# One layer of an eight-layer transformer kernel: last-token thoughts with features on partitions, token norms moved into the attention before, gates moved ahead of the thoughts

## The chip, the cores and the metric

The kernel runs on one core of a Trainium2 chip. The metric is the device time of one launch in microseconds (us), median over runs. All data is 32-bit floating point.

## What is computed

Eight layers on `x` of 4 batches x 256 tokens x 256 features, each added to `x` after a norm of it: cross-attention and feed-forward, four times (`a0 f0 a1 f1 a2 f2 a3 f3`). The change lies in `f1`, the second feed-forward layer, where a "thought" is made of each batch's last token and broadcast to all its tokens:

```python
def layer_norm(x, gamma, beta):
    mu = jnp.mean(x, axis=-1, keepdims=True)
    var = jnp.mean(jnp.square(x - mu), axis=-1, keepdims=True)
    return (x - mu) * jax.lax.rsqrt(var + EPS) * gamma + beta
x_norm = layer_norm(x, in_gamma, in_beta)
thought = x_norm[:, -1, :] @ agg_w + agg_b          # 4 x 256
for _ in range(4):
    t = layer_norm(thought, pn_gamma, pn_beta)
    t = gelu(t @ d1_w + d1_b)                        # 4 x 1024
    thought = thought + (t @ d2_w + d2_b)
broadcast = (thought @ bc_w + bc_b)[:, None, :]
gate = jax.nn.sigmoid(x @ gate_w + gate_b)
return layer_norm(x + gate * broadcast, out_gamma, out_beta)
# the caller: x = x + f1(_layernorm(x))
```

## The kernel before

The kernel is written on a tile framework. It places the tiles, sets every semaphore, and orders each engine's instructions ahead of time: a planner walks the program with its own cost estimates and gives an idle engine the first instruction, in the order of the source, that it thinks is ready. So the source order is a priority, later work fills gaps in earlier work, and the order is fixed before the chip runs. A tile of a pool waits until the memory, or the rotating buffer of its tag, is free.

`x` is held as eight tiles of 128 tokens x 256 features (two per batch), tokens on partitions. PSUM has 4 banks `work`, 3 `held` and one `longest`.

**The attention `a1`, before `f1`.** It goes through 4 batches x 16 heads x 2 token tiles. TensorE makes scores (`sc`), VectorE their maxima and ScalarE the exponentials, VectorE scales them, TensorE transposes them (`tp_a1p`) and multiplies with the context (`pv`) and the output weights (`o_a`, line 853). `finish` and `pair` trail the scores; `pair` is a generator in the list `left`, one step of which is taken per unit. At a batch's last head `pair` adds the batch's output to `x` (`add_to_x`, line 240).

**The layer `f1`.** Its weights (`f1w` with agg, bc and gate, `f1d1`, `f1d2`) are loaded long before. Then, in the order of the source:

1. Eleven vector loads (biases, gammas, betas; line 156), on 4 partitions for the thoughts and on 128 for the tokens.
2. `normed` normalizes all eight tiles (`normalizing`: two statistics instructions, `rsqrt` with a VectorE scale at line 177 and a GpSimd power at line 178, and one scaling at line 203) and transposes each into `xnT` (line 210).
3. Four small DMAs (line 1108) bring the four last tokens as rows to partitions 0 to 3 (`last`).
4. `layer_norm` on a 4 x 256 tile, `columns` (two transposes and a copy: features to partitions), the product with `agg`: `thought`, 4 x 256.
5. Four steps, each: `layer_norm`, `columns`, d1 (16 products that each hold a 128x128 block of weights and move 4 columns), bias (line 1140), Gelu (line 1145), d2 (8 products that hold 128x4 activations and move 256 columns of weights), two additions (1149, 1150).
6. The thought's columns, and per batch `same`, the product `bc` and `spread` (1160); per tile the gate's product, its bias (1165) and sigmoid (1166), then eight more VectorE steps (1168, 1169, the norm of `layer_norm` with 1112 and 1113, and 1171, the addition to `x`).

TensorE makes each 32-bit product in two passes, so two records of the trace are one product; a transpose is one record.

Between these stand the `weight_products` of the next attention `a2`: 28 short steps (`products`) on its weights, drawn with `drain(products, n)`: 4 behind each of the five norms of thoughts and 2 in each step between d1 and d2. A step is four transposes (of wk, wq, wv), or four products 128x128 (`a2wqk`), or one product of 512 columns (`a2wvo`), and a copy out of PSUM. Their weights come through two rotating buffers by DMA.

`a2` begins with `begin(0)`, which normalizes batch 0 again (`bn_a`, `xn_a`, `tp_a`), and then queries (`q_a`).

Of the kernel before, what the change touches and what calls it, by code (L numbers as in the profile page):

```python
# [10 lines left out]
F32 = mybir.dt.float32  # L11
# [43 lines left out]
class Model:  # L55
    def __init__(self, ctx: ExitStack, tc: tile.TileContext, aps, out, layers):
# [10 lines left out]

        self.early = ctx.enter_context(ExitStack())
        self.weights = self.early.enter_context(tc.tile_pool(name="weights", bufs=3))

        self.normal = ctx.enter_context(ExitStack())
        self.n_copies, self.kinds = 0, dict(work=("work", 4), held=("held", 4))
# [137 lines left out]
            self.nc.tensor.transpose(ps[:, n * w : (n + 1) * w], block, self.ident[:w, :w])  # L210
        self.copy(out, ps[:, : len(blocks) * w].rearrange("p (n w) -> p n w", w=w))

    def normed(self, tag, keep=None):

        xnT = []
        for c in range(NCH):
            xT = self.acts.tile([P, NK, CH], F32, tag="xnT", name=f"xnT_{tag}_{c}", bufs=2)
            for i in range(CH // P):
                n = c * (CH // P) + i
                if keep is None:  # L220
                    xn = self.acts.tile([P, D], F32, tag="xn", name=f"xn_{tag}_{n}", bufs=3)
                else:
                    xn = keep.tile([P, D], F32, tag="xn_kept", name=f"xn_{tag}_{n}", bufs=NT)
                    self.kept.append(xn)
# [405 lines left out]
    def f0(self):  # L630
# [5 lines left out]
        wg = self.load(self.w8([P, NK, I], "f0wg"), aps["L0_ffn_w_gate"].rearrange("(k p) n -> p k n", p=P))  # L636
        wu = self.load(self.w8([P, NK, I], "f0wu"), aps["L0_ffn_w_up"].rearrange("(k p) n -> p k n", p=P))
        wd = self.load(self.w8([P, NI, D], "f0wd"), aps["L0_ffn_w_down"].rearrange("(k p) n -> p k n", p=P))
        self.a1w = self.a1_weights()
        with tc.tile_pool(name="f0", bufs=2) as p, tc.tile_pool(name="f0a", bufs=1) as self.acts:  # L640
            xnT = self.normed("f0")
# [114 lines left out]
    def a1(self):  # L756
# [7 lines left out]
        NI = S // P  # L764
        wk, wv, wq, wvo, g = self.a1w
        self.share_banks(4)
        with self.tc.tile_pool(name="a1", bufs=2) as p:
            nc.vector.tensor_scalar_mul(g[:, 0:1], g[:, 0:1], 1.0 / math.sqrt(HD))

# [71 lines left out]
            def pair(b, h, wT):  # L841
# [235 lines left out]
        self.staging.close()  # L1077


    def f1(self):  # L1080
        nc, aps, tc = self.nc, self.aps, self.tc
        HID, STEPS = 1024, 4
        NH = HID // P
        EPS = 1e-6
        w = self.w8([P, 3, NK, D], "f1w")
# [3 lines left out]
        d2 = self.load(self.w8([P, NH, D], "f1d2"), aps["L1_ffn_d2_w"].rearrange("(k p) n -> p k n", p=P))  # L1089
        with tc.tile_pool(name="f1c", bufs=1) as cp, tc.tile_pool(name="f1", bufs=2) as p, tc.tile_pool(  # L1090
            name="f1st", bufs=2
        ) as st, tc.tile_pool(name="f1a", bufs=1) as self.acts:
            products = self.weight_products(st, "a2")
            self.ready.add("a2")
            rows = {}
            for name in ("in_gamma", "in_beta", "agg_b", "pn_gamma", "pn_beta", "d2_b"):
                rows[name] = self.load(cp.tile([B, D], F32, name=name), row(aps[f"L1_ffn_{name}"], B))
            for name in ("bc_b", "gate_b", "out_gamma", "out_beta"):
                rows[name] = self.load(cp.tile([P, D], F32, name=name), row(aps[f"L1_ffn_{name}"], P))
            d1b = self.load(cp.tile([P, NH], F32, name="d1b"), aps["L1_ffn_d1_b"].rearrange("(n p) -> p n", p=P))  # L1100

            self.kept = []
            xnT = self.normed("f1", keep=cp)
            xn = self.kept

            last = cp.tile([B, D], F32, name="last")
            for b in range(B):
                nc.sync.dma_start(last[b : b + 1, :], xn[(b + 1) * (S // P) - 1][P - 1 : P, :])

            def layer_norm(out, x, gamma, beta, name):  # L1110
                self.normalize(out, x, EPS, name)
                nc.vector.tensor_tensor(out, out, gamma, ALU.mult)
                nc.vector.tensor_tensor(out, out, beta, ALU.add)

            def columns(x, name):
                xT = p.tile([P, NK, B], F32, tag="xT", name=f"xT_{name}")
                self.transposed(xT, [x[:, k * P : (k + 1) * P] for k in range(NK)], name)
                return xT

            t = p.tile([B, D], F32, tag="t", name="t_in")  # L1120
            layer_norm(t, last, rows["in_gamma"], rows["in_beta"], "f1in")
            drain(products, 4)
            tT = columns(t, "f1in")
            thought = cp.tile([B, D], F32, name="thought")
            ps = self.held("agg")
            self.matmuls(ps[:B, :D], [(tT[:, k, :], w[:, 0, k, :]) for k in range(NK)])
            nc.vector.tensor_tensor(thought, ps[:B, :D], rows["agg_b"], ALU.add)
            for step in range(STEPS):
                t = p.tile([B, D], F32, tag="t", name=f"t_{step}")
                layer_norm(t, thought, rows["pn_gamma"], rows["pn_beta"], f"f1_{step}")  # L1130
                drain(products, 4)
                tT = columns(t, f"f1_{step}")
                ps = self.held(f"d1_{step}")
                for n in range(NH):
                    self.matmuls(
                        ps[:, n * B : (n + 1) * B],
                        [(d1[:, k, n * P : (n + 1) * P], tT[:, k, :]) for k in range(NK)],
                    )
# [12 lines left out]
            drain(products)  # L1151
            thT = columns(thought, "f1th")
            for b in range(B):

                same = p.tile([P, NK, P], F32, tag="same", name=f"same_{b}")
                nc.vector.tensor_copy(same, thT[:, :, b : b + 1].to_broadcast([P, NK, P]))
# [4 lines left out]
                for i in range(b * (S // P), (b + 1) * (S // P)):  # L1161
                    ps = self.work(f"gate_{i}")
                    self.matmuls(ps[:, :D], [(self.tokens(xnT, k, i * P, P), w[:, 2, k, :]) for k in range(NK)])
                    gate = p.tile([P, D], F32, tag="gate", name=f"gate_{i}")
                    nc.vector.tensor_tensor(gate, ps[:, :D], rows["gate_b"], ALU.add)
                    nc.scalar.activation(gate, gate, AF.Sigmoid)
                    o = p.tile([P, D], F32, tag="o", name=f"o_{i}")
                    nc.vector.tensor_tensor(o, gate, spread, ALU.mult)
                    nc.vector.tensor_tensor(o, o, xn[i], ALU.add)
                    layer_norm(o, o, rows["out_gamma"], rows["out_beta"], f"f1o_{i}")  # L1170
                    nc.vector.tensor_tensor(self.x[i], self.x[i], o, ALU.add)


    def clean_rows(self, p):
# [651 lines left out]
```

## Time and profile before

| | |
|---|---|
| median of 7 runs | 2581.31 us (2572.13 to 2584.39) |
| the profiled execution | 2581.88 us, span 2580.1 us |
| TensorE busy | 2402.8 us, 93% of the span |
| VectorE, ScalarE, GpSimd busy | 51%, 35%, 15% |
| mean granted TensorE clock | 0.938 |
| end of `a1`: its last addition to `x` starts | 1093.05 us |
| first `thought` (line 1127) | 1111.80 us |
| the thoughts' last addition (line 1150) ends | 1181.93 us |
| first query product `q_a` of `a2` | 1215.14 us |

The span runs from the first to the last instruction of the profile. "Busy" of TensorE counts pipelined products whose ends are modelled, so a busy TensorE need not be at its peak. The granted clock is the share of full speed that TensorE's throttle let through. Windows are given in us from the span's start. In a window's row each engine has its busy time and its number of instructions, PE is TensorE, PEld its weight loads, DVE VectorE, ACT ScalarE, POOL GpSimd, SP the queue that issues the DMAs.

### The profile page before, as it was taken

The page shows a single profiled execution, that of the slowest core. Times are in us where ns is not written, and L with a number is a line of the kernel's source. Part 1 is how long each engine was busy: PE and PEld are TensorE (multiplying, and loading weights), DVE is VectorE, ACT ScalarE, POOL GpSimd, SP SyncE. Part 2 cuts the span into 40 slices and gives each one's busy share as a digit, 9 for nine tenths or more (in the row PEclk, how much of TensorE's full clock was granted, in tenths as well). Part 3 has the DMA queues.
Part 4 walks back from the last instruction along what each step waited for, and adds up shares of the span by engine and source line. Part 5 has one row for each costly group of instructions (what it writes and reads, how often), then busy time and mean ns, then how long its engine had stood idle before and what let it go on. Part 6 is the DMA issues. An engine that isn't in the chain of part 4 may idle for free. (4 is left out here: it accounts for less than half of the span.)

```text
span 2580.1 us, 27636 instructions
## 1 busy us (share of the span) xinstructions
PE 2402.8 (93%) x9742; PEld 1436.2 (56%) x9742; DVE 1319.1 (51%) x3502; ACT 896.2 (35%) x1886; POOL 399.7 (15%) x412
## 2 busy tenths in 40 slices
PE   5999999898999999986999999898879999999999
PEld 3454545464555555553666666587746565654444
DVE  5453442686666666535566766311255666552111
ACT  2323322225555555411444344132334343431111
POOL 6303200002212121101001201100120201002222
PEclk8887875899999999977999999999989999999999
DMA  8400000200000000022200000199720000005111
GB/s 258 139 1 1 1 1 1 98 29 17 1 1 1 1 1 1 1 85 57 53 2 25 25 1 25 60 271 245 233 92 2 25 7 20 1 1 168 49 53 41
DMA packets 102422, 134.91 MB, mean 52 GB/s; under 512 B 8272, under 2 KB 82760, under 8 KB 101768
## 3 DMA queue, kind: packets, MB, share of 16 engines
q1 hardware_dynamic: 97672, 120.51, 15.7%
q0 software_dynamic: 4608, 12.59, 1.5%
q8 instruction: 79, 1.29, 0.2%
q14 instruction: 63, 0.52, 0.1%
HBM read 96.50 MB, written 36.57 MB: 52 GB/s over the span
## 5 line engine op out<-in xcount | busy, mean ns | idle before, releaser
L170 PE MATMUL pv_a<-PT_a,ctx 128*128 128x512 f32 x768 | 350.8, 600 | 4.8 <-DVE f3taken L1570 2.9
L998 DVE CUSTOM_DVE_ANT_0 pr_a<-sc_a,mask_a 128x512 f32<-128x512 f32 x256 | 176.2, 688 | 199.8 <-PE sc_a L170 199.3
L170 PE MATMUL sc_a<-ctxT,qT_a 128*128 128x512 f32 x512 | 261.6, 595 | 0.8 <-DVE sm_a L998 0.8
L170 PEld LDWEIGHTS pv_a<-PT_a,ctx 128*128 128x128 f32 x768 | 141.3, 190 | 189.4 <-issue 152.8
L999 ACT ACTIVATE pr_a<-pr_a,sm_a 128x512 f32<-128x512 f32 x256 | 185.0, 723 | 119.3 <-DVE sm_a L998 95.4
L178 POOL TENSOR_TENSOR rstd_f<-rs_f,half 128x1 f32<-128x1 f32 (+1 forms) x36 | 19.5, 568 | 880.0 <-DVE rs_f L177 679.9
L1004 DVE TENSOR_SCALAR pr_a<-pr_a,sm_a,valid_a 128x512 f32<-128x512 f32 x256 | 140.3, 551 | 5.9
L1461 DVE TENSOR_TENSOR h<-u,gs 128x512 f32<-128x512 f32 x48 | 33.2, 691 | 205.5 <-POOL gs L1459 205.2
L170 PE MATMUL sc_a<-kT,qT 128*128 128x512 f32 x256 | 131.2, 597 | 1.7 <-ACT qT L791 1.7
L170 PE MATMUL st<-qTm,a0kT 17*128 17x256 f32 x512 | 119.3, 544 | 11.6 <-ACT pT L573 10.1
L170 PE MATMUL sc_a<-a0kT,a0qz 128*128 128x496 f32 x256 | 123.7, 605 | 0.0
L517 DVE TENSOR_REDUCE a0pad<-sc_a 128x1 f32<-128x496 f32 x128 | 85.8, 672 | 72.9 <-PE sc_a L170 72.5
L825 ACT ACTIVATE pr_a<-sc_a,sm_a 128x512 f32<-128x512 f32 x128 | 87.8, 687 | 95.0 <-DVE sm_a L824 93.7
L178 POOL TENSOR_TENSOR rr_a1k<-rs_a1k,half 128x4 f32<-128x4 f32 x64 | 64.5, 1008 | 327.4 <-DVE rs_a1k L177 272.1
L165 DVE COPY xTb_f<-tp_xb_f 128x256 f32<-128x256 f32 x79 | 33.5, 424 | 141.6 <-PE tp_xb_f L210 141.6
L170 PEld LDWEIGHTS st<-qTm,a0kT 17*128 17x128 f32 x512 | 71.8, 254 | 58.8 <-ACT pT L573 36.9
L573 ACT ACTIVATE pT<-st 128x512 f32<-128x512 f32 x128 | 69.4, 594 | 95.4 <-PE st L170 95.1
L1458 ACT ACTIVATE gs<-g 128x512 f32<-128x512 f32 x48 | 28.7, 597 | 209.4 <-PE g L170 209.4
L210 PEld LDWEIGHTS tp_a3p<-ident,pr_a 128*128 128x128 f32 x512 | 63.9, 141 | 65.2 <-issue 50.0
L987 ACT COPY qT_a<-q_a 128x512 f32<-128x512 f32 x64 | 37.5, 586 | 178.1 <-PE q_a L170 178.1
L210 PEld LDWEIGHTS tp_a2p<-ident,pr_a 128*128 128x128 f32 x512 | 63.9, 141 | 61.8 <-issue 47.4
L210 PEld LDWEIGHTS tp_a1p<-ident,pr_a 128*128 128x128 f32 x512 | 63.8, 141 | 53.3 <-issue 44.6
(487 smaller groups left out, 4688.3 us busy)
## 6 DMA issues: line engine op xcount, KB each, us to landing
sent<-zero SPq DMA_DIRECT2D x6, 2048.0 KB
f2w<-in_L_w1T_dram SPq DMA_DIRECT2D x16, 704.0 KB
f2w<-in_L_w2T_dram SPq DMA_DIRECT2D x16, 704.0 KB
xb_f<-sent SPq DMA_DIRECT2D x20, 512.0 KB
back<-yb_f SPq DMA_DIRECT2D x20, 512.0 KB
cb_f<-f3comb SPq DMA_DIRECT2D x32, 192.0 KB
cb_f<-f3comb SPq DMA_DIRECT2D x32, 128.0 KB
f3wg<-in_L_wgT_dram SPq DMA_DIRECT2D x3, 1024.0 KB
```

Of the source, the lines that this page charges most:

```text
L165: self.nc.vector.tensor_copy(out, in_)
L170: self.nc.tensor.matmul(out, lhsT, rhs, start=n == 0, stop=n == last)
L178: self.last_pow = self.nc.gpsimd.tensor_tensor(out, t[:p, :n], self.half[:p, :n], ALU.pow).ins
L210: self.nc.tensor.transpose(ps[:, n * w : (n + 1) * w], block, self.ident[:w, :w])
L517: nc.vector.tensor_reduce(pad[:, h, HD : HD + 1], ps[:, :MAIN], AX.X, ALU.max, negate=True)
L573: nc.scalar.activation(pT[:, j], ps[j].rearrange("p (n t) -> p n t", n=2), AF.Exp)
L825: nc.scalar.activation(pr, ps, AF.Exp, bias=st[:, 0:1], accum_out=st[:, 1:2])
L987: nc.scalar.copy(qT, ps.rearrange("p (m t) -> p m t", m=2))
L998: nc.vector.tensor_tensor_reduce(pr, ps, mask, -1.0, -3 * NEG, ALU.add, ALU.min, accum_out=st[:, 0:1])
L999: nc.scalar.activation(pr, pr, AF.Exp, bias=st[:, 0:1], scale=-1.0, accum_out=st[:, 1:2])
L1004: nc.vector.tensor_scalar(pr, pr, st[:, 0:1], valid, ALU.mult, ALU.mult)
L1461: nc.vector.tensor_tensor(h, pu, t, ALU.mult)
```

## The change

- `f1_room`, called in `f0`, makes a pool that lives until the end of `f1`, with `xnT` and the eight normalized tiles. `f1_vectors`, called at the start of `a1`, loads the vectors: seven as columns (features on partitions), four as rows on 128 partitions.
- `f1_tokens(b)` normalizes and transposes batch `b`. For batches 0 to 2 it is put behind the last `pair` of the batch in `a1`'s list `left`; batch 3 follows at the start of `f1`.
- The gates (product, bias, sigmoid) of tiles 0 to 5 come before the transposes of batch 3, those of tiles 6 and 7 right behind; all are kept.
- The last tokens are copied out of `xnT` as columns by two VectorE copies; the four DMAs go.
- Thoughts have the form 128 x 2 x 4. A norm takes two pairs of products with a matrix of ones (sum, sum of squares, on every partition) in the place of the statistics instructions, and 2 product steps of `a2` behind each pair; `columns` goes. `agg` and d2 hold blocks of weights and move 4 columns, as d1 does. d2's bias is added before d2.
- `out_beta` is added to `x` by GpSimd before the thoughts; the last norm becomes two fused VectorE instructions.

```diff
...
+    def f1_tokens(self, b):
+        nc, NI = self.nc, S // P
+        self.f1_done.add(b)
+        xn = self.f1_xn[b * NI : (b + 1) * NI]
+        yield from self.normalizing_all(xn, b, f"f1_{b}")
...
+                nc.tensor.transpose(ps[:, k, i * P : (i + 1) * P], xn[i][:, k * P : (k + 1) * P], self.ident)
+        yield
+        self.copy(self.f1_xnT[c][:, :, at : at + S], ps)
+        yield
...
@@ a1, pair
+                    if b + 1 < B:
+                        left.append(self.f1_tokens(b))
...
@@ f1
-            self.kept = []
-            xnT = self.normed("f1", keep=cp)
-            xn = self.kept
-            last = cp.tile([B, D], F32, name="last")
-            for b in range(B):
-                nc.sync.dma_start(last[b : b + 1, :], xn[(b + 1) * (S // P) - 1][P - 1 : P, :])
-            def layer_norm(out, x, gamma, beta, name):
-                self.normalize(out, x, EPS, name)
-                nc.vector.tensor_tensor(out, out, gamma, ALU.mult)
-                nc.vector.tensor_tensor(out, out, beta, ALU.add)
...
+            def gate(i):
+                ps = self.work(f"gate_{i}")
+                self.matmuls(ps[:, :D], [(self.tokens(xnT, k, i * P, P), w[:, 2, k, :]) for k in range(NK)])
+                nc.vector.tensor_tensor(gates[i], ps[:, :D], rows["gate_b"], ALU.add)
+                nc.scalar.activation(gates[i], gates[i], AF.Sigmoid)
...
+            def sums(x, name):
+                ps = self.held(f"sums_{name}")
+                self.matmuls(ps[:, :B], [(self.ones, x[:, k, :]) for k in range(NK)])
+                return ps[:, :B]
+            def layer_norm(x, gamma, beta, name):
+                ps = sums(x, f"m_{name}")
+                drain(products, 2)
+                d, sq, t = tile_("d", name), tile_("sq", name), tile_("t", name)
+                nc.vector.scalar_tensor_tensor(d, each(ps), -1.0 / D, x, ALU.mult, ALU.add)
+                nc.vector.tensor_tensor(sq, d, d, ALU.mult)
+                ps = sums(sq, f"v_{name}")
+                drain(products, 2)
+                r = self.stats.tile([P, B], F32, tag="rr", name=f"rr_{name}")
+                self.rsqrt(r, ps, 1.0 / D, EPS, name)
+                nc.vector.tensor_tensor(d, d, over(gamma), ALU.mult)
+                nc.vector.tensor_tensor(t, d, each(r), ALU.mult)
+                nc.vector.tensor_tensor(t, t, over(beta), ALU.add)
+                return t
+            tokens = self.f1_tokens(B - 1)
+            drain(tokens, 2)
+            for i in range(NT - NI):
+                gate(i)
+            drain(tokens)
...
+            for i in range(NT - NI, NT):
+                gate(i)
+            for i in range(NT):
+                nc.gpsimd.tensor_tensor(self.x[i], self.x[i], rows["out_beta"], ALU.add)
...
+                nc.vector.tensor_tensor(thought, thought, over(cols["d2_b"]), ALU.add)
                 drain(products, 2)
                 ps = self.held(f"d2_{step}")
-                self.matmuls(ps[:B, :D], [(act[:, n, :], d2[:, n, :]) for n in range(NH)])
-                nc.vector.tensor_tensor(thought, thought, ps[:B, :D], ALU.add)
-                nc.vector.tensor_tensor(thought, thought, rows["d2_b"], ALU.add)
+                for f in range(NK):
+                    self.matmuls(
+                        ps[:, f * B : (f + 1) * B], [(d2[:, n, f * P : (f + 1) * P], act[:, n, :]) for n in range(NH)]
+                    )
+                nc.vector.tensor_tensor(thought, thought, by_half(ps), ALU.add)
...
-                    layer_norm(o, o, rows["out_gamma"], rows["out_beta"], f"f1o_{i}")
-                    nc.vector.tensor_tensor(self.x[i], self.x[i], o, ALU.add)
+                for i, o, mv, r in halves:
+                    nc.vector.scalar_tensor_tensor(o, o, mv[:, 0:1], rows["out_gamma"], ALU.subtract, ALU.mult)
+                    nc.vector.scalar_tensor_tensor(self.x[i], o, r, self.x[i], ALU.mult, ALU.add)
+        self.told.close()
```

More of the change, by code (lines that the diff above doesn't have):

```diff
@@ L766, in a1 @@
         self.share_banks(4)
+        self.f1_vectors()
         with self.tc.tile_pool(name="a1", bufs=2) as p:
@@ L1093, in f1 @@
             products = self.weight_products(st, "a2")
             self.ready.add("a2")
[L1095 to L1100, printed above, removed]
@@ L1115, in columns @@
[L1115 to L1124, printed above, removed]
-            ps = self.held("agg")
@@ L1126, in f1 @@
-            self.matmuls(ps[:B, :D], [(tT[:, k, :], w[:, 0, k, :]) for k in range(NK)])
-            nc.vector.tensor_tensor(thought, ps[:B, :D], rows["agg_b"], ALU.add)
+            gates = [cp.tile([P, D], F32, name=f"gate_{i}") for i in range(NT)]
+            def gate(i):
[3 more added lines that the diff above has]
+                nc.scalar.activation(gates[i], gates[i], AF.Sigmoid)
@@ new lines, in f1 @@
+            for i in range(NT):
+                nc.gpsimd.tensor_tensor(self.x[i], self.x[i], rows["out_beta"], ALU.add)
+            t = layer_norm(last, cols["in_gamma"], cols["in_beta"], "f1in")
+            thought = cp.tile(few, F32, name="thought")
+            ps = self.held("agg")
+            for f in range(NK):
+                self.matmuls(
+                    ps[:, f * B : (f + 1) * B], [(w[:, 0, k, f * P : (f + 1) * P], t[:, k, :]) for k in range(NK)]
+                )
+            by_half = lambda ps: ps[:, : NK * B].rearrange("p (f b) -> p f b", b=B)
@@ L1128, in f1 @@
+            nc.vector.tensor_tensor(thought, by_half(ps), over(cols["agg_b"]), ALU.add)
             for step in range(STEPS):
[L1129 to L1132, printed above, removed]
+                t = layer_norm(thought, cols["pn_gamma"], cols["pn_beta"], f"f1_{step}")
                 ps = self.held(f"d1_{step}")
@@ L1160, in f1 @@
                 nc.vector.tensor_tensor(spread, ps[:, :D], rows["bc_b"], ALU.add)
[L1161 to L1169, printed above, removed]
-                    layer_norm(o, o, rows["out_gamma"], rows["out_beta"], f"f1o_{i}")
-                    nc.vector.tensor_tensor(self.x[i], self.x[i], o, ALU.add)
+                halves = []
+                for i in range(b * NI, (b + 1) * NI):
+                    o = gates[i]
+                    nc.vector.tensor_tensor(o, o, spread, ALU.mult)
+                    nc.vector.tensor_tensor(o, o, self.f1_xn[i], ALU.add)
+                    bn = self.stats.tile([P, 6], F32, tag="bn", name=f"bn_f1o_{i}")
+                    mv = self.stats.tile([P, 2], F32, tag="mv", name=f"mv_f1o_{i}")
+                    r = self.stats.tile([P, 1], F32, tag="rstd", name=f"rstd_f1o_{i}")
+                    nc.vector.bn_stats(bn, o)
+                    nc.vector.bn_aggr(mv, bn)
+                    self.rsqrt(r, mv[:, 1:2], 1.0, EPS, f"f1o_{i}")
+                    halves.append((i, o, mv, r))
+                for i, o, mv, r in halves:
+                    nc.vector.scalar_tensor_tensor(o, o, mv[:, 0:1], rows["out_gamma"], ALU.subtract, ALU.mult)
+                    nc.vector.scalar_tensor_tensor(self.x[i], o, r, self.x[i], ALU.mult, ALU.add)
+        self.told.close()
     def clean_rows(self, p):
```

58 lines of the change are left out of this document (48 added, 10 removed).

## The prediction

> **What bounds the kernel now.** First the page's slices of 64.5 us: TensorE (PE) is at 9 tenths nearly everywhere, so elsewhere only PE work counts. Slices 17 and 18 (counted from 0; 1097 to 1226 us) dip to 8 and 6, at a granted clock of 7 tenths.
>
> ```profile
> PE   5999999898999999986999999898879999999999
> PEclk8887875899999999977999999999989999999999
> ```
>
> Second, the windows by stage: attention `a1`; its end to the first thought; the four steps; output to the first query of `a2`.
>
> ```profile
> core 0: us, PE busy (x) PEld busy (x) DVE busy (x) ACT busy (x) POOL busy (x), PEclk, DMA share, GB/s
> 650.00:1093.00 443.00, 432.54 (x1701) 252.10 (x1699) 295.18 (x685) 221.71 (x457) 84.25 (x88) 1.00 0.00 1
> 1093.00:1111.80 18.80, 10.90 (x42) 6.34 (x41) 11.05 (x35) 2.83 (x7) 2.66 (x5) 0.58 0.48 137
> 1111.80:1181.50 69.70, 64.31 (x316) 41.79 (x317) 18.61 (x50) 13.70 (x25) 2.12 (x4) 0.79 0.17 50
> 1181.50:1215.10 33.60, 12.43 (x49) 8.79 (x47) 28.88 (x110) 3.50 (x8) 6.28 (x12) 0.70 0.06 14
> ```
>
> Row 1: PE is full (432.5 of 443), VectorE (DVE) has a third free. Row 2: nobody is full; the thought waits for a chain of norm, DMAs and norm. Row 3: PE is nearly full, at clock 0.79. Row 4: DVE is the bound.
>
> Third, the clock inside a step, windows and then PE's timeline:
>
> ```profile
> 1116.90:1119.90 3.00, 3.00 (x30) 3.00 (x29) 0.28 (x1) 1.88 (x2) 0.00 (x0) 1.00 0.48 169
> 1119.90:1123.30 3.40, 3.40 (x18) 3.40 (x18) 0.53 (x2) 0.68 (x2) 0.00 (x0) 0.50 0.00 0
> 1123.30:1126.70 3.40, 3.40 (x12) 1.57 (x11) 0.69 (x1) 0.74 (x2) 0.00 (x0) 0.50 0.32 81
> 1126.70:1130.10 3.40, 3.40 (x20) 1.77 (x18) 0.82 (x2) 0.00 (x0) 0.00 (x0) 0.99 0.18 74
> ```
> ```profile
> 1116.86 4.04 PE L170 MATMUL d<-xT_f,f1d 128*128 128x4 f32 x32
> 1120.76 2.05 PE L170 MATMUL a2wqk<-a2wkT,a2wqT 128*128 128x128 f32 x8
> 1122.61 1.92 PE L210 MATMUL tp_a2wq<-ident,a2wq 128*128 128x128 f32 x8
> 1124.45 4.73 PE L170 MATMUL d<-f1d,act 128*4 128x256 f32 x16
> ```
>
> d1, products that move 4 columns, fills PE without a gap from 1116.86, yet at 1119.9 the clock halves. d2, which moves 256 columns, starts at 1124.45 and has it back at 1126.7. The trace's starts give the price: records of d1 come every 0.112 us at full clock, 0.213 at half; of d2 every 0.216 and 0.427. The clock changes on a grid of 3.41 us (1113.1, and two and four such stretches later 1119.9 and 1126.7). A cold stretch turned warm with 2.25 of its 3.41 us in products of 256 columns (1123.3 to 1126.7), not with 1.85 in 128-column products and 0.7 in transposes (1119.9 to 1123.3). All three other stretches filled by d1 dropped the clock too.
>
> **The change, part by part**, against the profiled execution's 2581.88 us (span 2580.1), 0.57 over the median.
>
> *Tokens in the attention.* Three batches put 12 transposes on a full PE: 12 x 0.11 (record spacing, full clock) = 1.3 us; with a wait now and then +1.6 (0.5 to 4). Their norms (per tile statistics 0.41 + 0.17, scale 0.15, scaling 0.41) take 7 us on DVE, copies and powers 2 and 3 us: free in row 1. Eleven loads move to SP at `a1`'s start, 0.3 to 0.4 us of issue each; nothing behind them is wanted for 400 us. Without that cover they would cost the 4.8 us that they take now (1093.08 to 1097.75). GpSimd (POOL) adds `out_beta` eight times, 0.81 us each by the 128x256 row at L454; six fit in `a1`, two (1.6 us) lie before the first norm's power while POOL idles.
>
> *Attention's end to the first thought*, now 1093.05 to 1111.80 = 18.75 us. After: gates 0 to 5 on a warm PE, 6 x 4 x 0.216 = 5.2 us, over batch 3's norm on DVE (ready at 3.5); transposes, copy 0.6 and `last` to 6.7; gates 6 and 7, 1.7, to 8.2. They stand ahead of the thoughts in PE's queue, so the first sums wait for them. The norm and `agg`: 16 small records 1.8, links off PE 2.6, two pairs of transpose steps 1.8 less 0.6 hidden: 5.6 warm, up to 2.5 more cold. First thought at 13.8 warm; I take 13.9, since the gates have just kept the clock up. Gain 4.85 (2 to 5.5). The products' weights are now asked for at 0, not 7.9, and land in time (3.9 us for `a2wk`).
>
> *The four steps*, 1111.80 to 1181.93 = 70.1. New PE work per step: 8 records of sums, 32 of d1, 32 of d2, all moving 4 columns: 72 x 0.112 = 8.1 warm, 72 x 0.213 = 15.3 cold. d2 alone costs what it did (16 x 0.216 against 32 x 0.112), but no longer moves 256 columns. Links off PE, from small rows (128x32 addition 0.19, Gelu 0.23, scale 0.14): addition 0.25; difference and square 0.44; scale, power and two operations 1.77; bias and Gelu 0.53; four waits for a product's end at 0.18: 3.7. The power is on 128x4 now, 1.01 us, not 0.53:
>
> ```profile
> L178 POOL TENSOR_TENSOR rr_a1q<-rs_a1q,half 128x4 f32<-128x4 f32 x32 | 32.2, 1007 | 106.8 <-DVE rs_a1q L177 101.3 <-DVE rs_a L177 5.5
> L178 POOL TENSOR_TENSOR rstd_f<-rs_f,half 4x1 f32<-4x1 f32 x4 | 2.1, 531 | 60.0 <-DVE rs_f L177 60.0
> ```
>
> So a bare step is 11.8 warm, 19.0 cold. 24 product steps stand in the four: 32 transposes (0.11 / 0.213), 64 records of `a2wqk` (0.112 / 0.213), 16 of `a2wvo` (0.43 / 0.99 as seen): 17.6 warm, 36.2 cold. Of that 11 to 12 hide in the links; the rest stands ahead of the next sums, d1 or d2 in PE's queue. All warm: 47 + 17.6 - 11 = 54. All cold: 76 + 36.2 - 12 = 100. The same sum with the old records gives 53 and 95; the measured 70.1 lies 59% of the way to warm.
>
> Which clock? Only `a2wqk` and `a2wvo` can raise it now: eight pairs of steps, each about 3.4 us cold. One that starts anywhere on the grid has 2.25 us in one stretch in 2 x (3.41 - 2.25) / 3.41 = 68% of cases, and buys one warm stretch, worth 3.41 less the links' share: 2.9. 8 x 0.68 x 2.9 = 16, so 84. Two more for copies of products that sit ahead of the chain on DVE (0.5 us a step now, as the 0.69 us copy at 1114.65 before L1113): 86. Cost 15.9; ends 75 (each pair raises it for a full 3.41) and 102 (none does).
>
> Here a rule can be weighed. The Trainium skill, "TensorE: Matmul & The Clock Gate", Part 1 (The HAM clock gate), has the clock halve after about 3.4 us without PE activity and advises against idle gaps. The grid agrees; "idle" does not, since PE was busy 3.00 of 3.00 us before the drop. By the rule a PE full of small products would stay warm and the steps would take 54 + 2, a gain of 14; I go by the row.
>
> *Output.* DVE now, 1184.5 to 1212.6:
>
> ```profile
> L1171 DVE TENSOR_TENSOR x<-x,o 128x256 f32<-128x256 f32 x8 | 3.3, 416 | 0.0
> L1112 DVE TENSOR_TENSOR o<-o,out_gamma 128x256 f32<-128x256 f32 x8 | 3.3, 414 | 0.0
> L1165 DVE TENSOR_TENSOR gate<-gate,gate_b 128x256 f32<-128x256 f32 x6 | 2.4, 401 | 0.0
> ```
>
> Such instructions of 0.41 start 0.335 apart. Per tile four (L203, L1112, L1113, L1171) become two fused ones; the fused row at L1244 takes 0.48, I put 0.40 (0.335 to 0.48) apart: 4 x 0.335 - 2 x 0.40 = 0.54, x 8 = 4.3. Six gate biases go: 2.0. The thought's transposes and copy go (1.0), a cold first `bc` takes half back: 0.5. Gain 6.8 (5 to 9); after it the start of `a2` is late next, as now.
>
> **Sum:** +1.6 - 4.85 + 15.9 - 6.8 = +5.85: 2587.7, less 0.57 for the median: **2587**.
>
> **The rivals.** About 0.2% (5.2 us) is what a measurement of this kernel can tell from no change.
>
> *The clock stays up (faster).* The mechanism: pairs of products, or gates which the planner pulls into the steps as it now does at 1174.96, raise the clock in nearly every stretch. It decides where the steps take under 75 us, 27 of the 46 between cold and warm. For it: `a2wvo` pairs move 512 columns and follow each other in step four. Against: a 128-column run of 1.85 us failed, and gates stand first. Price: 2557 (all warm) to 2576, typically 2572.
>
> *Paid back exactly (same).* 17 to 27 of the 46 saved, steps 75 to 85: 2576 to 2586, middle 2581. Nothing in the rows excludes that six pairs of eight land well on a grid whose phase I do not know.
>
> *Small products leave the clock cold (slower).* My case: steps over 85. With no raise at all and an attention 4 us longer, 2605. That tokens in `a1` delay `pair` more than 4 us would add to it; row 1 has 10 us idle in 443, so some is absorbed.
>
> **How the numbers follow.** Slower 0.5, same 0.3, faster 0.2: I trust the count of cold records, less how the pairs fall. My case's own range is 2587 to 2604. Over all, 2570 to 2604: below, long raises with the better ends of attention and output (steps 75: -5; ends -5); above, one raise in eight.
>
> **What would show it.** Right: records of d2 0.213 apart with a granted clock of 0.5 to 0.7 in the steps; first thought 14 us after the last addition of `a1`; thoughts 82 to 90 us; last `x` some 20 us after the last thought; `a1` 1 to 2 us longer. Wrong: a clock of 0.79 or more in the steps, or d2 records 0.112 apart throughout, or an attention longer by over 5 us.

## The result, and the profile after

The median after is 2591.87 us (19 runs, 2581.76 to 2598.77) beside 2581.31 before (45 runs): a ratio of 1.0043 with a 95% interval of 1.0033 to 1.0054, so 8.5 to 13.9 us slower. The profiled execution took 2592.74 us (span 2591.0) against 2581.88.

The page's slices first, in tenths, 64.8 us each: PE is at 9 and 7 tenths in slices 17 and 18 now, while the clock is still down there, at 7 and 6.

```profile
PE   5999999898999999997999999898869999999999
PEclk7897875899999999976999999999989999999999
```

The windows by stage, cut at the same events as those of before (attention, its end to the first thought, the four steps, output to the first query of `a2`):

```profile
core 0: us, PE busy (x) PEld busy (x) DVE busy (x) ACT busy (x) POOL busy (x), PEclk, DMA share, GB/s
650.00:1105.40 455.40, 437.88 (x1721) 257.26 (x1720) 303.51 (x702) 223.12 (x461) 90.41 (x97) 0.99 0.00 1
1105.40:1119.00 13.60, 12.13 (x80) 10.78 (x79) 11.03 (x35) 6.05 (x12) 3.55 (x5) 1.00 0.43 145
1119.00:1197.00 78.00, 75.37 (x387) 66.92 (x386) 10.97 (x45) 11.08 (x20) 4.04 (x4) 0.65 0.16 45
1197.00:1221.70 24.70, 7.82 (x20) 4.83 (x20) 22.14 (x88) 0.59 (x1) 7.26 (x13) 0.60 0.14 43
```

Against the stages before (18.75, 70.1 and 33.2 us) the start is 5.2 shorter, the steps are 7.9 longer at a clock of 0.65, and the output is 8.6 shorter. The three batches of the attention between the first and the last addition to `x` took 125.9 + 126.0 + 105.1 us before and take 128.6 + 131.0 + 108.7 now. With 1.1 us before any of the moved work, the attention ends 12.4 us later.

12.4 - 5.2 + 7.9 - 8.6 = 6.5. The other 4.3 of the profiled 10.9 lie behind the first query: from the end of `a2` to the first addition of `a3` it takes 6.6 us longer (386.0 before, 392.6 after), and what follows takes some 2.5 less. In the fourteen traces of this study this stretch is 379.7 to 392.8 long, with nothing of the change in it and no order by kernel, so it is laid to the single execution. The medians are 8.5 to 13.9 us apart all the same. What 6.5 lacks is probably in the attention: the five other kernels that keep it as it is after the change (3, 8, 9, 11 and 12 below) take 371.6 us for the three batches, not 368.4, and 6.5 + 3.2 = 9.7.

**Where the attention waits.** PE's timeline behind the second batch turn (start, duration, line, tiles; in brackets the idle time and its releaser):

```profile
873.67 0.60 PE L1112 MATMUL tp_f<-ident,f1xn 128*128 128x128 f32 x4
874.11 0.60 PE L211 MATMUL tp_a1p<-ident,pr_a 128*128 128x128 f32 x4
877.78 1.11 PE L789 MATMUL t_a1q<-ident,nrm_a1q 128*128 128x128 f32 x4 [3.08 <-DVE nrm_a1q L783]
```

PE idles 3.08 us for the normalized queries of the next heads. Behind the three turns it idles 2.38, 3.08 and 3.08 us, where before no idle time of over 0.2 us stands in the first 15 us behind a turn. DVE's timeline says why:

```profile
865.75 0.74 DVE L237 TENSOR_TENSOR x<-x,o_a 128x256 f32<-128x256 f32 x2
867.01 0.74 DVE L200 BATCH_NORM_STATS2 bn_f<-x 128x6 f32<-128x256 f32 x2
...
871.51 0.69 DVE L783 TENSOR_TENSOR nrm_a1q<-ps_a1q,rr_a1q 128x512 f32<-128x512 f32 x1 [0.98 <-POOL rr_a1q L179]
872.12 1.36 DVE L204 TENSOR_SCALAR f1xn<-x,mv_f,rstd_f 128x256 f32<-128x256 f32 x2
...
873.58 0.98 DVE L830 TENSOR_SCALAR pr_a<-pr_a,sm_a 128x512 f32<-128x512 f32 x1
874.49 0.67 DVE L778 TENSOR_REDUCE ss_a1q<-sq_a1q 128x4 f32<-128x512 f32 x1
...
877.04 0.69 DVE L783 TENSOR_TENSOR nrm_a1q<-ps_a1q,rr_a1q 128x512 f32<-128x512 f32 x1 [0.61 <-POOL rr_a1q L179]
```

The second `nrm_a1q` starts 11.3 us after the additions to `x`; before, it starts 8.4 us after them (870.22 against 861.86). The same turn before the change, and its end in kernel 4 below, where the scalings lie elsewhere and the additions are at 868.78:

```profile
862.60 0.41 DVE L199 BATCH_NORM_STATS2 bn_f<-x 128x6 f32<-128x256 f32 x1
870.22 0.69 DVE L784 TENSOR_TENSOR nrm_a1q<-ps_a1q,rr_a1q 128x512 f32<-128x512 f32 x1 [1.19 <-POOL rr_a1q L178]
```
```profile
878.20 0.69 DVE L783 TENSOR_TENSOR nrm_a1q<-ps_a1q,rr_a1q 128x512 f32<-128x512 f32 x1 [0.59 <-POOL rr_a1q L179]
```

The statistics (`bn_f`) are not what opens the gap: the planner had put those of batches 0 to 2 behind the turns in the kernel before too, and in kernel 4 they stand ahead of both sums of squares `ss_a1q`, with the second `nrm_a1q` 9.4 us behind the additions and PE idle for 0.42 us. What is new between the two query tiles are the scalings (`f1xn`, 1.36 us) and a `pr_a` scaling of 0.98 us, not 0.49, beside POOL's addition. Then the idle PE pays twice, in the windows during and behind the gap:

```profile
874.70:877.80 3.10, 0.02 (x2) 0.02 (x1) 2.49 (x6) 1.26 (x3) 1.02 (x1) 0.99 0.00 0
877.70:881.20 3.50, 3.42 (x10) 2.28 (x11) 2.34 (x6) 1.36 (x3) 0.00 (x0) 0.51 0.02 5
881.20:884.70 3.50, 3.50 (x14) 1.78 (x13) 2.63 (x9) 1.96 (x5) 0.00 (x0) 1.00 0.00 0
```

The stretch that follows runs at a clock of 0.51. The same happens behind the third turn (0.60), not behind the first. That is chance: in kernels 3, 8, 9, 11 and 12, with the same gap of 2.38 us, the clock is down for 3.41 us behind the first turn too, and the batch takes 130.3 us, not 128.7. So a cold stretch costs 1.7 us. There are two behind the turns in this trace, four in those.

**In the steps** PE's timeline shows 32 records of d1 or d2 at both clocks: 3.7 us warm, 6.8 us cold.

```profile
1122.75 3.74 PE L171 MATMUL d<-t_f,f1d 128*128 128x4 f32 x32 [0.27 <-DVE t_f L1172]
1128.93 6.83 PE L171 MATMUL d<-act,f1d 128*128 128x4 f32 x32
1183.79 3.71 PE L171 MATMUL d<-t_f,f1d 128*128 128x4 f32 x32 [0.15 <-DVE t_f L1172]
```

d2 is cold in steps one to three and in half of step four. By the last additions to `thought` the steps take 16.9, 17.7, 23.0 and 20.5 us. Windows of 3.41 us from 1119.0 on show the two longest warm parts end, the first in step one, the second in step four:

```profile
1122.41:1125.83 3.42, 3.15 (x29) 3.08 (x28) 0.25 (x2) 1.61 (x2) 0.00 (x0) 1.00 0.49 148
1125.83:1129.24 3.41, 3.41 (x23) 3.41 (x23) 0.19 (x1) 1.41 (x3) 0.00 (x0) 0.66 0.02 5
...
1183.85:1187.26 3.41, 3.41 (x32) 3.41 (x32) 0.52 (x1) 0.00 (x0) 0.00 (x0) 1.00 0.25 85
1187.26:1190.67 3.41, 2.80 (x16) 2.71 (x16) 0.19 (x1) 0.23 (x1) 0.00 (x0) 0.66 0.00 0
```

A clock of 0.66 in such a window is a third of it warm: the clock falls at 1127 and at 1188.4.

**In the output** DVE's groups have two fused instructions where four stood:

```profile
L1247 DVE SCALAR_TENSOR_TENSOR x<-gate,rstd_f1o,x 128x256 f32<-128x256 f32 x8 | 3.9, 484 | 0.1
L1246 DVE SCALAR_TENSOR_TENSOR gate<-gate,mv_f1o,out_gamma 128x256 f32<-128x256 f32 x8 | 3.6, 463 | 0.0
```

### The profile page after: what moved, and what is told of

Read it like the earlier page. It is cut to its first block, busy times and chain, and to the rows that moved or that the text cites. A ratio compares the mean times of both kernels' runs of the same rounds, so it can differ in the third digit from the quotient of the medians.

```text
span 2591.0 us, 27808 instructions
## 1 busy us (share of the span) xinstructions
PE 2420.3 (93%) x9838; PEld 1471.7 (57%) x9838; DVE 1309.9 (51%) x3483; ACT 895.2 (35%) x1881; POOL 408.8 (16%) x420
## 3 DMA queue, kind: packets, MB, share of 16 engines
q1 hardware_dynamic: 99128, 120.49, 15.9%
## 5 line engine op out<-in xcount | busy, mean ns | idle before, releaser
L179 POOL TENSOR_TENSOR rstd_f<-rs_f,half 128x1 f32<-128x1 f32 x32 | 17.3, 555 | 819.6 <-DVE rs_f L178 652.2
L1538 DVE TENSOR_TENSOR h<-u,gs 128x512 f32<-128x512 f32 x48 | 33.2, 691 | 205.5 <-POOL gs L1536 205.1
```

Source lines behind the costliest of these rows:

```text
L179: self.last_pow = self.nc.gpsimd.tensor_tensor(out, t[:p, :n], self.half[:p, :n], ALU.pow).ins
```

## The experiments

Theory A: the attention lost because the moved norm stands ahead of the query chain in DVE's queue at the batch turn. Theory B: POOL's additions of `out_beta` did it. Theory C: what keeps PE's clock up is the columns that products stream, not the records that fill PE. The runs were made on three chips. The one of kernels 5 to 8 takes about 20 us longer in `a2`, outside the changed stages, with every kernel that was profiled there; so kernels are compared by their ratio to the kernel before in the same session, and by the stages ahead of `a2`. Stage times are from one profiled execution each, in us; "start" is the attention's last addition to the first thought, "batches" the three of the attention.

| kernel | batches | start | steps | clock in steps | output | ratio to before (95%) |
|---|---|---|---|---|---|---|
| before | 357.1 | 18.8 | 70.1 | 0.79 | 33.2 | 1 |
| after | 368.4 | 13.6 | 78.0 | 0.65 | 24.6 | 1.0043 (1.0033 to 1.0054) |
| 1 tokens late | 359.3 | 15.0 | 80.4 | 0.62 | 25.6 | 0.9981 (0.9968 to 0.9994) |
| 2 `out_beta` late | 364.9 | 14.1 | 78.4 | 0.63 | 25.6 | 1.0009 (0.9992 to 1.0026) |
| 3 wide products | 371.6 | 14.0 | 53.7 | 1.00 | 24.7 | 0.9934 (0.9912 to 0.9955) |
| 4 tokens mid-batch | 360.4 | 13.5 | 79.8 | 0.62 | 24.6 | 0.9999 (0.9981 to 1.0016) |
| 5 before, d1 wide | 357.1 | 17.2 | 58.6 | 0.97 | 33.2 | 0.9976 (0.9963 to 0.9990) |
| 6 = 2 + 3 + 4 | 360.4 | 14.5 | 53.8 | 1.00 | 24.7 | 0.9903 (0.9885 to 0.9921) |
| 7 = 1 + 3 | 359.3 | 15.0 | 57.1 | 0.94 | 24.7 | 0.9896 (0.9879 to 0.9913) |
| 8 d2 wide alone | 371.6 | 13.8 | 65.8 | 0.79 | 24.6 | 0.9962 (0.9932 to 0.9991) |
| 9 gates late | 371.6 | 12.8 | 79.8 | 0.64 | 27.5 | 1.0053 (1.0034 to 1.0072) |
| 10 = 7, gates in the steps | 359.3 | 12.3 | 59.8 | 1.00 | 24.7 | 0.9912 (0.9886 to 0.9938) |
| 11 32 columns | 371.6 | 13.5 | 74.3 | 0.68 | 25.6 | one run: 2579.78 us |
| 12 16 columns | 371.6 | 13.6 | 80.0 | 0.62 | 25.6 | one run: 2592.61 us |

### 1. Tokens late

```diff
-                    if b + 1 < B:
-                        left.append(self.f1_tokens(b))
```

> The tokens of batches 0 to 2 are normalized and transposed at the start of f1, none in the attention; POOL's out_beta additions come behind them too. Theory A (the moved tokens are what made the attention 12.4 us longer): the last addition to x of a1 starts at 1093 to 1095, as in the kernel before, not 1105.5; the three batches take 126, 126 and 105 us again; from there to the first thought it takes 18 to 22 us, not 13.6, since six more tiles wait for DVE (about 1 us each) before the gates. Time against the kernel after: -3 to -8 us, so 2584 to 2589. Rival (the longer attention has another cause, such as the pool that holds the tiles or the loads at its start): a1 still ends at 1103 or later, and the time is 2595 to 2600.

Measured: batches 125.9, 126.0 and 107.3; the last addition at 1097.4 (the batch before the first moved norm also ended 2.1 later than in the kernel before); first thought 15.0 later. The groups of the query transposes between 738 and 1010 us, over all three turns (busy us, mean ns of one, then the idle time before them and its releaser), of this kernel and then of the kernel after:

```profile
L789 PE MATMUL t_a1q<-ident,nrm_a1q 128*128 128x128 f32 x72 | 10.8, 273 | 0.0
```
```profile
L789 PE MATMUL t_a1q<-ident,nrm_a1q 128*128 128x128 f32 x72 | 12.0, 292 | 9.5 <-DVE nrm_a1q L783 9.5
```

No idle time is left before them. The moved tokens are the cause; the rival falls. (Their statistics stay behind the turns, where the planner puts them in the kernel before; what is gone are the powers, scalings, transposes and POOL's additions.) The expectation was wrong about what it costs to have them late: 1.4 us at the start, not 4 to 8, because the planner pulled the scalings into the last batch, from 1063.9 on, where they lengthened it by 2.2. The ratio fell by 0.62%, about 16 us, more than the 3 to 8 expected. The stages ahead of `a2` give 9.1 in the batches less 1.4 at the start, 2.4 in the steps and 1.0 in the output; 8 us lie in the stretch behind `a2`, which varies between executions. With the 371.6 us that the attention takes in the other kernels like after, the batches would give 12.3. How much of the rest belongs to the edit is not settled.

### 2. `out_beta` late

```diff
-                nc.gpsimd.tensor_tensor(self.x[i], self.x[i], rows["out_beta"], ALU.add)
+                inst = nc.gpsimd.tensor_tensor(self.x[i], self.x[i], rows["out_beta"], ALU.add).ins
+                tc.add_manual_dep(inst, self.last_pow.name, ORDER, reason="batch 3's norm is wanted first")
```

> As the kernel after, but POOL adds out_beta to x only behind the powers of batch 3's norm, so none of these additions lies in the attention. Theory A (the moved norm stands ahead of the q chain in DVE's queue): the attention stays long, a1's last addition at 1102 to 1105 (at most 3 us earlier, which is two DVE instructions of 0.4 to 0.5 us that took 0.9 to 1.0 beside each pair of POOL additions, three times), PE gaps of 2 us or more ahead of the q transposes remain behind the batch turns; time 2588 to 2592. Theory B (POOL's additions beside DVE make the loss): a1 ends at 1096 or earlier, no gap over 1 us; time 2580 to 2584.

Measured: gaps of 2.10 us behind all three turns (2.38, 3.08, 3.08 in the kernel after); batches 128.4, 130.1, 106.4; last addition at 1103.9. The long wait stays, as theory A has it. But POOL's additions were worth more than the 3 us allowed: 3.5 against the trace of after, 6.7 against kernels 3, 8 and 9, whose batches sum to 371.6. Most of that is the clock: behind the turns there is one cold stretch here, two in after, four in those three. At 1.7 us for each, the additions themselves were worth about 1.8 us against either.

### 3. Wide products

```diff
+            wide = lambda x, r: x.unsqueeze(1).to_broadcast([P, r, B])
...
-                self.matmuls(ps[:, :B], [(self.ones, x[:, k, :]) for k in range(NK)])
+                self.matmuls(ps[:, :P].rearrange("p (r b) -> p r b", b=B), [(self.ones, wide(x[:, k, :], 32)) for k in range(NK)])
...
-                        ps[:, n * B : (n + 1) * B],
-                        [(d1[:, k, n * P : (n + 1) * P], t[:, k, :]) for k in range(NK)],
+                        ps[:, n * 64 : (n + 1) * 64].rearrange("p (r b) -> p r b", b=B),
+                        [(d1[:, k, n * P : (n + 1) * P], wide(t[:, k, :], 16)) for k in range(NK)],
...
```

d2 is done as the sums, 32 times; the additions behind d1 and d2 read the first 4 columns of each block.

> As the kernel after, but each small product moves its 4 columns over and over: sums 32 times (128 columns), d1 16 times (64), d2 32 times (128); the additions read the first 4. Theory C (what keeps the clock is columns streamed, not records in PE's queue): records of d1 and d2 0.112 us apart in most of the steps, granted clock 0.9 or more there, the steps 54 to 62 us, not 78.0, and the time 2568 to 2576. Rival (the clock falls for another reason, such as the waits between the links): clock 0.65 as before, records 0.213, steps 76 to 82, time 2590 to 2596.

The window of its four steps:

```profile
1122.80:1176.50 53.70, 50.12 (x390) 44.77 (x389) 10.75 (x45) 11.07 (x20) 4.03 (x4) 1.00 0.24 72
```

Full clock throughout, 53.7 us: the "all warm" sum of the prediction was 54. Theory C stands: the same instructions, in the same number, take 24 us less because each streams more columns. At full clock 32 records of d1 take 3.76 us with 64 columns and 3.74 with 4, so the additional columns are free.

### 4. Tokens mid-batch

```diff
-                    if b + 1 < B:
-                        left.append(self.f1_tokens(b))
...
+                if hg == 1 and b > 0:
+                    steps = itertools.chain(steps, self.f1_tokens(b - 1))
```

> As the kernel after, but the moved tokens of a batch come in the second quarter of the heads of the next batch (with the steps of prepare for the third), not right behind the batch's last addition. Theory A (their place, ahead of the q chain behind the turn, is what costs): no PE gap over 1 us behind the turns, a1's last addition at 1094 to 1098, the three batches 126 to 128, 126 to 128 and 105 to 107 us; time 2581 to 2586. Rival (the work itself, on a PE that is full and a DVE that has less room than it seems, costs wherever it is put): a1 ends at 1102 or later, time 2589 to 2593.

Measured: batches 127.4, 127.4 and 105.6, no gap over 0.7 us behind a turn. They are 1.5, 1.4 and 0.5 longer than before: 3.3 us in sum, which is what the moved work costs on a PE that is full. The end at 1101.8 says less than the batches do, since the first batch, ahead of all moved work, ended 5.4 us later than in the kernel before. The statistics stay behind the turns; the powers, scalings, transposes and POOL's additions (from 784.4 on) lie mid-batch, and no cold stretch follows. So 8.0 us of the 11.3 were the place, two cold stretches of 1.7 us among them.

### 5. The kernel before with d1 wide

```diff
-                        ps[:, n * B : (n + 1) * B],
-                        [(d1[:, k, n * P : (n + 1) * P], tT[:, k, :]) for k in range(NK)],
+                        ps[:, n * 64 : (n + 1) * 64].rearrange("p (r b) -> p r b", b=B),
+                        [(d1[:, k, n * P : (n + 1) * P], wide(tT[:, k, :], 16)) for k in range(NK)],
```

> The kernel before with one edit: d1 moves its 4 columns 16 times over (64 columns). Theory C (columns streamed keep the clock): d1 no longer drops the clock, records of d1 0.112 us apart, clock 0.95 or more, the four steps 53 to 59 us in the place of 70.1 (the all-warm sum of the prediction with the old records was 53); time against before -11 to -17 us. Then the kernel before could have had most of what the wide products bring, without features on partitions. Rival (64 columns do not suffice, or the long links of the old norm let the clock fall): steps 66 to 71 us, time within 4 us of before.

The window of its steps:

```profile
1116.10:1174.80 58.70, 52.67 (x320) 35.95 (x320) 19.03 (x51) 13.58 (x25) 2.12 (x4) 0.97 0.21 65
```

Clock and steps came as theory C has them, 11.5 us less. The one cold stretch follows 2.43 us in which PE waited for a DMA. The whole kernel gained 2.6 to 9.7 us by its interval, less than the 11 to 17 expected; since the kernel before was not profiled on that chip, where the missing part lies stays open.

### 6 and 7. Edits together

> As the kernel after, with three edits together: tokens in the second quarter of the next batch, POOL's out_beta additions behind the last norm's power, and all small products wide. If their effects add, the batches of a1 take 126 to 128, 126 to 128 and 105 to 107 us, the steps 53 to 56, and the time is 2556 to 2563; if tokens at mid-batch cost as much as behind the turn, 2565 to 2570.

> As the kernel after, with two edits: no tokens in the attention (they come at the start of f1) and all small products wide. If the effects of the two single edits add (steps 78.0 to 53.7, that is -24; tokens late -8 to -13 against the kernel after): 2553 to 2559 us, about 1.0% below the kernel before; batches of a1 126, 126 and 105 to 107 us, steps 53 to 55. Rival (a warm start of f1 was bought by the tokens' place, or f2, which waits for its transfers, takes back what is gained ahead of it): 2562 us or more.

Times are to be read through the ratios here, the kernel before being at 2609.1 us in that session: 0.9903 and 0.9896 of 2581.3 are 2556.3 and 2554.5, both where the sum of single effects was expected. Both beat both kernels. The batches of number 6, with no addition of `out_beta` in the attention, are those of number 4 to a tenth, so away from the turn POOL's additions cost nothing. Steps of 57.1 in number 7 miss the expected 53 to 55: its clock was 0.94, not 1.00.

### 8. d2 wide alone

```diff
-                        ps[:, f * B : (f + 1) * B], [(d2[:, n, f * P : (f + 1) * P], act[:, n, :]) for n in range(NH)]
+                        ps[:, f * P : (f + 1) * P].rearrange("p (r b) -> p r b", b=B),
+                        [(d2[:, n, f * P : (f + 1) * P], wide(act[:, n, :], 32)) for n in range(NH)]
```

Sums and d1 keep 4 columns.

> As the kernel after, but d2 alone moves 128 columns (its 4, 32 times); sums and d1 still move 4. The step of the prediction that is tested: d2 with 4 columns in the place of 256 is what lost the clock. If d2 alone is enough to keep it most of the time: steps 58 to 68 us and a clock of 0.8 to 0.95, time -10 to -20 against after. If d1 and the sums drop it anyway, as d1 did in the kernel before: steps 69 to 76, clock 0.65 to 0.8.

```profile
1126.90:1192.70 65.80, 62.39 (x386) 54.96 (x385) 10.93 (x45) 10.96 (x20) 4.03 (x4) 0.79 0.17 51
```

Steps of 65.8 at a clock of 0.79, exactly the clock of the kernel before. (0.8 to 0.95 was expected.) So d2's step from 256 columns to 4 is what took the clock from 0.79 to 0.65; d1 and the sums hold it at 0.79.

### 9. Gates late

```diff
-            for i in range(NT - NI):
-                gate(i)
...
                 for i in range(b * NI, (b + 1) * NI):
+                    gate(i)
                     o = gates[i]
```

> As the kernel after, but the gates stand where the kernel before has them, per tile in the output (their order on PE, among the thoughts, is the planner's). The prediction put them at 5.2 us of PE ahead of the first sums and took 2.0 us off the output for the biases. If that holds: a1's last addition to the first thought 10 to 12.5 us, not 13.6 (the gates no longer stand ahead, batch 3's norm and transposes then end last); steps 72 to 78 (256-column products of gates that the planner pulls in raise the clock once or twice), the output 27 to 29 us, not 24.6; time within 4 us of after. Rival (gates in front keep the clock for the start and pulling them apart costs it): first thought at 14 us or later, time 4 to 8 us above after.

First thought at 12.8 (10 to 12.5 expected), steps 79.8 (72 to 78 expected), output 27.5. Gates in front cost the start 0.8 us and save the output 2.9. The rival's loss of clock is there too: without gates the clock is down from 1112.2 to 1119.0, 0.73 over the start against 1.00 in the kernel after, so the 0.8 is net of that. The planner put no gate among the steps: the first gate product starts at 1199.3, as they end. So this run does not test whether gates there raise the clock.

### 10. Gates inside the steps

On top of kernel 7, the gates ahead of the thoughts go, and in each step there are two:

```diff
                 drain(products, 2)
+                for i in range(step * NI, (step + 1) * NI):
+                    gate(i)
                 ps = self.held(f"d2_{step}")
```

> Tokens late, all small products wide, and two gates between d1 and d2 of each step in the place of eight ahead of the thoughts. If PE has room in the steps' links: first thought 10 to 12.5 us after a1's last addition (14.7 with gates ahead), steps 57 to 61 (53.7 and 57.1 with gates ahead), output 24 to 26; about 1.0% below the kernel before, within 0.2% of the version with tokens late and wide products alone. If PE has no room there: steps 61 to 65, and the version with gates ahead is faster by 0.1 to 0.3%.

Start 12.3 against 15.0, steps 59.8 against 57.1: what one stage gains the other pays, and the ratios' intervals overlap. No difference is shown.

### 11 and 12. How many columns

The edits of experiment 3 with all small products at 32 columns (`wide(..., 8)`) and at 16 (`wide(..., 4)`):

```diff
-                        ps[:, n * B : (n + 1) * B],
-                        [(d1[:, k, n * P : (n + 1) * P], t[:, k, :]) for k in range(NK)],
+                        ps[:, n * 32 : (n + 1) * 32].rearrange("p (r b) -> p r b", b=B),
+                        [(d1[:, k, n * P : (n + 1) * P], wide(t[:, k, :], 8)) for k in range(NK)],
```

> As the kernel after, with the small products moving 32 columns each (4 columns, 8 times). Where the turn lies between 4 columns (clock 0.65, steps 78.0) and 64 to 128 (clock 1.00, steps 53.7): theory C with a share of streamed time of about a third as the bound for staying warm puts 32 columns near it, steps 54 to 70, clock 0.75 to 1.0. A theory in which only the number of busy cycles counts expects no change from 4 columns: 76 to 80.

> As the kernel after, with the small products moving 16 columns each. Theory C: too little to stay warm, steps 70 to 80, clock 0.63 to 0.75, above the kernel with 32 columns by 5 us or more; if 16 already suffice, steps under 60.

```profile
1120.70:1195.00 74.30, 71.97 (x386) 63.94 (x385) 10.73 (x45) 11.06 (x20) 4.03 (x4) 0.68 0.15 46
```
```profile
1120.70:1200.60 79.90, 77.81 (x386) 69.66 (x385) 10.68 (x45) 11.06 (x20) 4.03 (x4) 0.62 0.14 42
```

16 columns do nothing (a clock of 0.62, 0.63 to 0.75 expected), 32 hardly anything (steps of 54 to 70 and a clock of 0.75 to 1.0 expected). The single time of the kernel with 32, 2579.78, owes more to the stretch behind `a2`, 379.7 us in that execution, the shortest of all. At 0.84 ns a column (256 in 0.216 us) a record of 0.112 us streams for 24% of its time with 32 columns, 48% with 64. The point at which a stretch full of small products stays warm lies between these two.

The fourteen traces give it more closely. From 1090 to 1240 us, cut each into stretches of 3.41 us on the grid of its clock's changes, and count the columns that PE's records move in each stretch, a transpose as 128. Of 356 stretches at full clock, all with 1583 columns or more kept it, and all with 1449 or fewer lost it. Of 246 at half clock, all with 1505 or more raised it, and of those with 1490 or fewer only one did (1485). So here about 1500 columns in a stretch decide the clock of the next, whatever the clock is now. At 0.112 us a record, some 30 records fill a stretch: 960 columns with 32 each, 1920 with 64. It also explains kernel 7's 0.94: its loss follows a stretch of 1432 columns, in which PE waited 0.96 us. The count is an estimate, since a trace can lack some records, and holds for these products: before 470 us, where many hold only 17 rows of weights, stretches of over 4000 columns left the clock down.

## Why the prediction was right, and where not

The total, 2587 against 2591.87, was right in sign and within the range, but two of its terms were off in opposite directions, by +10.8 and -8.0 us. That they nearly cancel is luck: with the attention as predicted, the stages measured here would sum to -4.3, and the kernel would have come out in the band of the rival "paid back exactly".

**The attention is the term that was mis-sized: +1.6 (0.5 to 4) against +12.4.** The step that failed is the cover: "free in row 1". DVE had a third of its time free over 443 us, and POOL most of it, but the moved norm was put at the batch turn, where the query chain is queued and PE waits for it. There is no slack there, and 2 to 3 us of idle PE behind each turn brought cold stretches with them. Of the 7 us of DVE work that the term counted, the statistics were no new work: the planner had them in the attention before. Mid-batch the same work cost 3.3 us (experiment 4), inside the range given. POOL's additions were counted as nothing; at the turn they were worth about 1.8 us, and 3.5 to 6.7 with the cold stretches (experiment 2), elsewhere nothing (6). The prediction named this as its sign of being wrong, "an attention longer by over 5 us", and as an unpriced tail of its slower case, but not the mechanism.

**The steps: +7.9 against +15.9 (ends 75 and 102).** The mechanism was right: records 0.213 apart with a clock of 0.65. The term that was off is the number of warm stretches. The prediction counted 5.4 stretches (8 x 0.68), 18.6 us, all of them raised by pairs of products; the granted clock of 0.65, between 0.5 cold and 1.0 warm, means 30% of the 78 us warm, 23.5. The clock was still up from the start until 1127, 8 us that the sum had at nothing, and it was raised four times, not 5.4, once for 6.8 us (two `a2wvo` pairs in a row before step four's d1). Whether the gates left it up is not shown: without them (9) the steps begin warm too, until 1125.8. At 0.85 us gained per warm us, 100 - 0.85 x 23.5 = 80. The 2 us added for copies ahead of the chain on DVE are then not needed. At 78.0 the steps alone fell into the band of the rival "paid back exactly"; the slower outcome is the attention's.

**Start and output** were right: 13.6 against 13.9, and a gain of 8.6 against 6.8 (5 to 9). Of the latter DVE's busy time gave 28.88 - 22.14 = 6.7, which is what the prediction added up. Its idle time in the window gave 2.1 more (4.7 to 2.6), which no term had: before, DVE waited 1.9 us for POOL's powers, and after, with the norms of two tiles side by side, it does not.

```profile
L203 DVE TENSOR_SCALAR o<-o,mv_f1o,rstd_f1o 128x256 f32<-128x256 f32 x8 | 3.3, 412 | 2.1 <-POOL rstd_f1o L178 1.9
```

Of the gates' 5.2 us of PE ahead of the first sums only 0.8 came back when they were moved away, with a clock that then fell (9).

**The rule and the row.** The Trainium skill, "TensorE: Matmul & The Clock Gate", Part 1 (The HAM clock gate), says that the gate goes by how busy PE has been over a window of about 3.4 us. Experiment 12 had PE busy 77.81 of 79.90 us and a clock of 0.62; experiment 3 had it busy 50.12 of 53.70 and 1.00. Busy as the profile counts it is not what the clock follows; the columns moved (11 and 12) tell the two apart.

## What to carry to other kernels

Before work is moved onto an engine that is "a third free", look at the queue at the very place where it will stand, and at who waits behind it: the same norm cost 3.3 us in the middle of a batch and 11.3 at its turn, cold stretches included. When a product is turned so that it moves 4 columns in the place of 256, count streamed columns, not instructions (here some 1500 in 3.41 us kept the clock); where such products fill PE, repeating their columns up to the free 64 or 128 kept the clock and took the steps from 78.0 to 53.7 us.

## What the runs showed of the hardware

- A PE that is busy with small products can be cold: clock 0.62 to 0.68 at 4, 16 and 32 columns, 1.00 at 64 and 128, with records of the same length at full clock (3.74 and 3.76 us for 32).
- A DVE scaling beside a POOL addition takes about half a microsecond longer. In the window behind the second turn, the scalings of the kernel after, and then those of the kernel with `out_beta` late (four and four in a group: busy us, mean ns):

```profile
L830 DVE TENSOR_SCALAR pr_a<-pr_a,sm_a 128x512 f32<-128x512 f32 x4 | 2.4, 607 | 0.1
```
```profile
L830 DVE TENSOR_SCALAR pr_a<-pr_a,sm_a 128x512 f32<-128x512 f32 x4 | 1.9, 482 | 0.1
```

One of the four took 0.98 us beside POOL's 0.73 us addition. The Trainium skill, "SBUF — State Buffer", section "SBUF: two separate sides", says that GpSimd shares one pair of ports with VectorE instructions in a two-port mode or with two inputs in SBUF, and that the one that starts first holds the pair to its end. A delay of 0.5 us agrees with that in kind; that this scaling is such an instruction no run here shows.
